# A tile ahead of the tile pools made 64 bytes longer, in a gated recurrence with a binary-weight feed-forward layer

## The chip, the cores and the metric

The kernel runs on one core of a Trainium2 chip. The metric is the time of one execution on the device in microseconds. The core's engines are TensorE (PE in the profile; its weight loads stand apart as PEld), VectorE (DVE), ScalarE (ACT), GpSimd (POOL) and SyncE (SP), which here only issues DMAs. SBUF, the memory that the engines work on, has 128 partitions; a tile takes the same range of bytes in each of them.

## The reference

The input x is [2, 4096, 256] in float32. Each of two layers is added to its input and normalised over the last axis. Cut to what matters:

```python
u = x @ W_in + b_in                       # 64 state columns
g = sigmoid(x @ W_gate + b_gate)
h_t = tanh(h_prev @ A + u_t @ Bm)         # over 4096 steps
y_t = h_t @ C.T + u_t @ D.T
y_t = g_t * y_t + (1 - g_t) * x_t
x1 = layernorm(x + (ys @ W_out + b_out + x))
# binary weights: sign(w) times the mean of |w| over a row
f = gelu(x1 @ bw1.T + b1) @ bw2.T + b2    # 256 -> 1024 -> 256
out = layernorm(x1 + f)
```

## The kernel before

**Work.** The 4096 steps of each of the two sequences are cut into 64 segments of 64 steps, so that 128 recurrences run side by side. A warm-up of 48 steps gives each segment its first state. After the run the states are compared with those that they started from; where they differ, a branch at L757 computes the recurrence one step after another and redoes all chunks. `hs`, the tile of the change, serves that branch alone.

**Chunks.** The rows are worked in 16 chunks of 512 (`N`). For each chunk the method `load` fetches `hu` (states and inputs, from `st` in SBUF) and `xn` (x, from memory); `xt` is x transposed, loaded on its own. Then follow the gate products (L313), `mix` (L370, then VectorE at L377, L382, L385), `project` (L395), the first normalisation, and `turn` (transposes at L423). `turn` splits the result into a rounded part `xhi` (ScalarE, L431) and the remainder `xlo` (VectorE, L433), both in the float32r type. `up` (L451) multiplies the signs `sg1` with both parts; the Gelu at L458 evicts the sums to `h`, which ScalarE and VectorE split again into `hhi` (L467) and `hlo` (L474). `down` (L490) uses these as weights against the signs `sg2`. The end of a chunk is `scale` (L506), `add` (L512), the second normalisation and the store (L527). An up product streams 512 columns, a down product 256. The step of the recurrence is L157 on TensorE and L158 on ScalarE; L131 makes its inputs u.

**Order.** The order of the instructions on TensorE, ScalarE, VectorE and GpSimd is written out by hand in a manual schedule. Each chunk's pieces stand among those of its neighbours, and a step of the recurrence is put in after every so many nanoseconds of planned work. SP issues nearly all DMAs, in the order of the code.

**Where tiles stand.** The pools take bytes of a partition in the order in which they are opened: `const`, `xin`, `work`, `small`. Each tile of a pool stands at a fixed byte. In the built program the `const` pool holds `st`, all weights and constants, and as its last tile `hs`; behind it come `xin` (`xt`, `hu`, `xn`), `work` (`tg`, `h`, `xhi`, `xlo`, `hhi`, `hlo`, `d`, `o`, and for a time w1, w2 and the `neg` tiles of the sign computation) and `small` (the statistics of the normalisations). A tile starts on a multiple of 32 bytes at the least. The large tiles of `const`, such as `sg1`, `sg2`, `cd`, `w_gate`, `w_out` and `wab`, start on multiples of 128 bytes.

```python
cp = ctx.enter_context(tc.tile_pool(name="const", bufs=1))
xp = ctx.enter_context(tc.tile_pool(name="xin", bufs=2))
wk = ctx.enter_context(tc.tile_pool(name="work", bufs=2))
sm = ctx.enter_context(tc.tile_pool(name="small", bufs=4))
...
hs = cp.tile([P, L + 1 + 7, B], FP, name="hs")
```

Here P is 128, L is 64 and B is 2: in each partition `hs` has 72 rows of two float32 numbers. The branch uses the first 65 of them.

Of the kernel before, what the change touches and what calls it, by code (L numbers as in the profile page):

```python
# [8 lines left out]
FP = mybir.dt.float32  # L9
# [7 lines left out]
P = 128  # L17
B, T, DM, S, H = 2, 4096, 256, 64, 1024
# [3 lines left out]
L = T // SEG  # L22
# [15 lines left out]
def gated_recurrence_then_binary_ffn(  # L38
# [18 lines left out]
    cp = ctx.enter_context(tc.tile_pool(name="const", bufs=1))  # L57
# [694 lines left out]
        do(end, "down_end")  # L752


    hs = cp.tile([P, L + 1 + 7, B], FP, name="hs")
    met = nc.values_load(flag, min_val=0, max_val=B * S * (SEG - 1))
    with tc.If(met < B * S * (SEG - 1)):  # L757
        nc.vector.memset(hs[TOP, L, :], 0.0)
# [58 lines left out]
```

## Time and profile before

| | us |
|---|---|
| median of three runs | 452.75 |
| lowest, highest | 452.65, 454.31 |
| the profiled execution | 453.36 |
| its span | 451.5 |
| TensorE busy | 439.7 |
| VectorE busy | 358.0 |
| ScalarE busy | 261.1 |
| GpSimd busy | 176.2 |

The span runs from the first instruction to the last; the profiled execution's own time holds a little more around it. Busy time is the time in which an engine had an instruction in work. Matmuls overlap in the profile, since one starts before the one ahead of it has ended; the distance from start to start tells their rate better than their length. The chain that ended last is followed back from the last instruction, at each step to what released it, and is shown in pieces of like instructions; there each piece lasts up to the start of what follows it.

### The profile page before, as it was taken

How to read it: one execution, taken by the hardware profiler on the slowest of the kernel's cores; microseconds unless marked ns; L12 is line 12 of the kernel's file. 1: busy time of each engine (PE TensorE's matmuls, PEld its weight loads, DVE VectorE, ACT ScalarE, POOL GpSimd, SP SyncE). 2: the span in 40 equal slices, each digit the busy share in tenths (PEclk: the TensorE clock that was granted, in tenths of full speed). 3: DMA queues.
4: the chain of work that ended last, by engine and by line, in shares of the span. 5: the costliest groups of instructions: out<-in, count | busy, mean ns of one | idle time of the engine just before them, and what ended most of it. 6: DMA issues, size and time to landing. Idle time of an engine off the chain costs nothing.

```text
span 451.5 us, 6729 instructions
## 1 busy us (share of the span) xinstructions
PE 439.7 (97%) x2504; PEld 357.6 (79%) x2504; DVE 358.0 (79%) x600; ACT 261.1 (58%) x424; POOL 176.2 (39%) x179
## 2 busy tenths in 40 slices
PE   8999999999999999999999999999999999989992
PEld 5665666788888888887978787979788888879982
DVE  0245737976989798989898988899898989896775
ACT  2343442485657575757574747566666656556772
POOL 1001300553545434343445454535353545451713
PEclk9999999999999999999999999999999999999997
DMA  8898814321133322322232312212112020201012
GB/s 302 267 330 305 292 36 137 102 83 23 48 105 106 107 59 94 116 94 70 93 103 70 105 52 89 76 52 67 47 37 81 13 93 1 93 1 48 1 46 100
DMA packets 14838, 44.51 MB, mean 99 GB/s; under 512 B 2000, under 2 KB 3024, under 8 KB 14800
## 3 DMA queue, kind: packets, MB, share of 16 engines
q1 hardware_dynamic: 14224, 43.65, 29.1%
q8 instruction: 22, 0.36, 0.3%
q10 hardware_dynamic: 576, 0.37, 0.3%
q14 instruction: 16, 0.13, 0.1%
HBM read 31.43 MB, written 8.39 MB: 88 GB/s over the span
## 4 chain that ended last, share of the span: by engine, by line
PE 92%; DVE 5%; DMA 1%; ACT 1%; issue 0%; POOLq 0%; POOL 0%
PE ps_h L451 25%; PE ps_o L490 24%; PE ps_z L395 12%; PE ps_g L313 12%; PE ps_y L370 6%; PE ps_s L157 6%; PE ps_u L131 4%; PE ps_t L423 3%; DMA wab<-in_W_in_AB 1%; DVE bs_b L256 1%; DVE hlo L474 1%; DVE d L382 1%; DVE d L377 1%; DVE xlo L433 1%; DVE o L506 0%; PE ps_p L490 0%
## 5 line engine op out<-in xcount | busy, mean ns | idle before, releaser
L458 ACT ACTIVATE h<-ps_h,bias_c,al 128x512 f32<-128x512 f32 x128 | 97.5, 775 | 80.4 <-PE ps_h L451 75.2
L490 PE MATMUL ps_o<-sg,hhi 128*128 128x256 f32 x496 | 120.3, 282 | 0.0
L490 PE MATMUL ps_o<-sg,hlo 128*128 128x256 f32 x496 | 119.0, 279 | 0.1
L474 DVE TENSOR_TENSOR hlo<-h,hhi 128x1024 fp32r<-128x1024 f32 (+1 forms) x65 | 84.5, 1318 | 23.6 <-ACT hhi L467 23.5
L490 PEld LDWEIGHTS ps_o<-sg,hhi 128*128 128x128 f32 x496 | 93.6, 189 | 2.3
L490 PEld LDWEIGHTS ps_o<-sg,hlo 128*128 128x128 f32 x496 | 93.4, 188 | 2.5 <-DVE hlo L474 0.3
L451 PE MATMUL ps_h<-xhi,sg 128*128 128x512 f32 x256 | 92.2, 441 | 0.0
L451 PE MATMUL ps_h<-xlo,sg 128*128 128x512 f32 x256 | 80.2, 394 | 0.2
L355 POOL TENSOR_TENSOR xn<-xn,bo_r 128x256 f32<-128x256 f32 x64 | 59.3, 957 | 48.4 <-DMA xn<-in_x 48.4
L355 POOL TENSOR_TENSOR xn<-xn,b_r 128x256 f32<-128x256 f32 x64 | 75.5, 1208 | 1.2 <-PE ps_t L423 1.2
L467 ACT CAST hhi<-h 128x1024 fp32r<-128x1024 f32 (+1 forms) x65 | 67.3, 1037 | 2.0
L313 PE MATMUL ps_g<-xt,w_gate 128*128 128x384 f32 (+3 forms) x208 | 67.9, 438 | 0.0
L266 POOL TENSOR_TENSOR rs_a<-rs_a,neg_half 128x4 f32<-128x4 f32 x16 | 17.2, 1076 | 122.2 <-DVE rs_a L265 103.4
L395 PE MATMUL ps_z<-w_out,tg 128*128 128x256 f32 x256 | 61.1, 380 | 1.5 <-DVE xlo L433 1.5
L158 ACT ACTIVATE st<-ps_s 64x128 f32<-64x128 f32 x112 | 30.0, 267 | 56.0 <-PE ps_s L157 55.6
L451 PEld LDWEIGHTS ps_h<-xlo,sg 128*128 128x128 f32 x256 | 48.1, 188 | 11.9 <-DVE xlo L433 0.9
L157 PEld LDWEIGHTS ps_s<-st,wab 128*128 128x128 f32 x224 | 38.0, 192 | 24.0 <-issue 9.9
L451 PEld LDWEIGHTS ps_h<-xhi,sg 128*128 128x128 f32 x256 | 46.1, 189 | 12.7 <-issue 6.2
L266 POOL TENSOR_TENSOR rs_b<-rs_b,neg_half 128x4 f32<-128x4 f32 (+1 forms) x19 | 19.3, 1017 | 89.2 <-DVE rs_b L265 77.0
L395 PEld LDWEIGHTS ps_z<-w_out,tg 128*128 128x128 f32 x256 | 46.0, 190 | 6.8 <-DVE xlo L433 1.7
L279 ACT ACTIVATE xn<-xn,nm_a,rs_a 128x256 f32<-128x256 f32 x60 | 31.2, 591 | 24.5 <-DVE nm_a L271 24.5
L157 PE MATMUL ps_s<-st,wab 128*128 128x128 f32 x224 | 44.6, 281 | 0.1
(73 smaller groups left out, 482.9 us busy)
## 6 DMA issues: line engine op xcount, KB each, us to landing
xt<-in_xT SPq DMA_DIRECT2D x35, 512.0 KB, 4.3
xn<-in_x SPq DMA_DIRECT2D x16, 512.0 KB, 3.4
out_y<-xn SPq DMA_DIRECT2D x15, 512.0 KB, 2.6
hu<-st SPq DMA_DIRECT2D x32, 128.0 KB, 2.3
w1t<-in_w1T SPq DMA_DIRECT2D x2, 512.0 KB, 5.9
w1n<-in_w SPq DMA_DIRECT2D x2, 512.0 KB, 6.1
w2t<-in_w2T SPq DMA_DIRECT2D x2, 512.0 KB, 4.9
xt<-in_xT SPq DMA_DIRECT2D x2, 256.0 KB, 3.5
```

Source lines behind the costliest of these rows:

```text
L157: nc.tensor.matmul(p_h, ab, st[:, j].rearrange("p b k -> p (b k)"), start=True, stop=True)
L158: nc.scalar.activation(h_of[:, j + 1].rearrange("p b k -> p (b k)"), p_h[TOP, :], AF.Tanh)
L266: nc.gpsimd.tensor_tensor(rs, rs, neg_half[:, cut], ALU.pow)
L279: nc.scalar.activation(r, r, AF.Identity, bias=self.sh[:, i : i + 1], scale=rs)
L313: nc.tensor.matmul(ps[:, cut], w_gate[:, k, bass.ts(m, P)], xt_[:, k, cut], start=k == 0 and i == 0, stop=k == KD - 1, skip_group_check=True,)
L355: nc.gpsimd.tensor_tensor(r[:, i, :], r[:, i, :], row, ALU.add)
L395: nc.tensor.matmul(self.ps_z[:, i, :], self.y[:, k, bass.ts(i, P)], w_out[:, k, :], start=k == 0, stop=k == KD - 1,)
L451: nc.tensor.matmul(ps, sg1[:, k, bass.ts(j, P)], part[:, k, :], start=n == 0, stop=n == 2 * KD - 1,)
L458: nc.scalar.activation(h[:, i, :], ps, AF.Gelu, bias=b1_c[:, j : j + 1], scale=al1[:, j : j + 1],)
L467: nc.scalar.copy(hi[:, part, :], h[:, part, :])
L474: nc.vector.tensor_sub(lo[:, i, :], h[:, i, :], hi[:, i, :].bitcast(FP))
L490: nc.tensor.matmul(ps[:, i, :], part[:, j % 2, bass.ts(tb, P)], sg2[:, j, :], start=j == 0 and part is self.h[j // 2][0] and first, stop=j ...
```

## The change

The tile `hs` gets 15 rows of padding in place of 7. It is 640 bytes long in each partition in place of 576, and all tiles of `xin`, `work` and `small` stand 64 bytes higher.

```diff
-    hs = cp.tile([P, L + 1 + 7, B], FP, name="hs")
+    hs = cp.tile([P, L + 1 + 15, B], FP, name="hs")
```

## The prediction

> **What bounds the kernel now.** I read the page's busy table and its slices first, then the chain that ended last, then the waits, then single stretches.
>
> ```profile
> PE 439.7 (97%) x2504; PEld 357.6 (79%) x2504; DVE 358.0 (79%) x600; ACT 261.1 (58%) x424; POOL 176.2 (39%) x179
> ...
> PE   8999999999999999999999999999999999989992
> ...
> DMA  8898814321133322322232312212112020201012
> ...
> PE 92%; DVE 5%; DMA 1%; ACT 1%; issue 0%; POOLq 0%; POOL 0%
> ```
>
> TensorE is busy in 97% of the span and in every slice but the last, and it is 92% of the chain that ended last. DMA is dense only in the first five slices. Busy matmul time alone proves little, since matmuls overlap; so the waits of TensorE come next.
>
> ```profile
> PE ps_z L395 <- DVE xlo L433: 1.5, 1, 1.5
> PE ps_s L154 <- POOL ones L107: 1.0, 1, 1.0
> PE ps_u L131 <- DMA wab<-in_W_in_AB: 0.4, 1, 0.4
> PE ps_y L370 <- DVE d L377: 0.2, 1, 0.2
> ```
>
> The columns are total us, times, longest us. In all, TensorE waits 3.1 us. No x tile that comes by DMA is among what it waits for, in spite of the dense first five slices. So a change must alter the rate of TensorE itself, or the few microseconds at either end, to be seen. The rate is in the pieces of the chain between 390 and 440 us (start, length, what):
>
> ```profile
> 404.90 1.89 PE ps_o L490 x16
> 408.51 1.85 PE ps_h L451 x8
> 410.36 1.84 PE ps_o L490 x16
> ...
> 430.02 3.73 PE ps_h L451 x16
> ```
>
> The same sixteen down products take 1.89 us in one piece and 1.84 us in another. Among the 34 pieces of exactly sixteen in the chain's longest pieces I count 22 of 1.89, 11 of 1.84 and one of 1.88: mean 1.8735 us, 117.1 ns a product. In the timeline of single products, starts at 414.46 and 415.14 us stand six products apart, 113.3 ns each; those at 213.16 and 214.93 us stand fifteen apart, 118.0 ns each. **TensorE has two paces** for these products, and changes between them without any wait. An up product (512 columns) takes 230.6 ns in a piece of eight at 1.845 us, and 233 ns in the piece of sixteen.
>
> **What the Trainium skill says.** "SBUF — State Buffer", section "Operand start alignment", asks only that an operand start at a multiple of its element size, and says of its runs that they "timed nothing": no price for 64 against 128 bytes. The same page, "Specifications (TRN2)", speaks of 16-byte lines; 64 and 128 are both multiples of 16, so by it no engine access changes. Its "Who interferes with whom" gives TensorE two independent read ports, moving operand and weights, and says that it never waits on anyone; the two paces show that something still costs 4.7 ns a product. "DMA: Bandwidth & Descriptors", "How a descriptor splits into AXI transactions", says that transactions start at multiples of 256 bytes. No row here shows a transaction; the 3.5 us that a first half of xt took to land is used below.
>
> **The change part by part.** The built programs place `hs` at byte 77184 of each partition in both. It is 576 bytes long before and 640 after, so `xin`, `work` and `small` begin at 77760 (607 x 128 + 64) before and at 77824 (608 x 128, also 19 x 4096) after. Tiles of `xin` and `work` take 2048 or 4096 bytes, so each starts 64 bytes past a multiple of 128 before and on one after. The statistics of `small` (slots of 96 and 32 bytes) keep mixed starts, whatever the title says. The `const` tiles do not move. Every engine's and queue's list of instructions has the same order: nothing is removed, added or moved past anything, SP's and POOL's included, and no wait is added.
>
> (1) `hs` itself is used only in the branch at L757, which did not run: no row of the profile has a line of it. Cost 0.
>
> (2) TensorE's reads. The kernel before already holds both cases. The down products stream `sg2` (a `const` tile, on a multiple of 128) against weights from `hhi`/`hlo` (64 past one); the up products stream `xhi`/`xlo` (64 past) against weights from `sg1` (on one). Per 512 columns the first are 2 x 117.1 = 234.2 ns, or 226.6 at the fast pace; the second 230.6. The tiles 64 past are not slower. Weight loads take the same from either:
>
> ```profile
> L490 PEld LDWEIGHTS ps_o<-sg,hhi 128*128 128x128 f32 x496 | 93.6, 189 | 2.3
> ...
> L451 PEld LDWEIGHTS ps_h<-xhi,sg 128*128 128x128 f32 x256 | 46.1, 189 | 12.7 <-issue 6.2
> ```
>
> So I take 0, by the nearest rows. What the trace does not hold is an up or down product with both of its streams on multiples of 128. Bounds for that: all down products at the fast pace give 64 sixteens x (1.8735 - 16 x 0.1133) = 3.9 us less; all at the slow pace 64 x (1.89 - 1.8735) = 1.1 us more, and all up products at 233 ns another 512 x 2.4 ns = 1.2 us, together 2.3 us more.
>
> (3) VectorE, ScalarE, GpSimd. VectorE gives the pair to compare:
>
> ```profile
> L195 DVE TENSOR_SCALAR nega<-w1t 128x512 f32<-128x512 f32 x4 | 1.7, 420 | 0.0
> ...
> L188 DVE TENSOR_SCALAR w_out<-w_out 128x512 f32<-128x512 f32 x1 | 0.4, 427 | 0.0
> ```
>
> 420 ns on pool tiles against 427 on a `const` tile, of one size: no gain from a multiple of 128. ScalarE's casts take 1051 ns for 1024 elements and 616 for 512, 0.85 ns an element, and VectorE's `hlo` row of 512 takes 688 ns, 1.34 ns an element with its start. There is no such pair for ScalarE or GpSimd; were each 5% off either way, it would lie under TensorE, whose products wait 1.7 us in all for VectorE and never for ScalarE. I take 0, and 0.3 us either way for the tail after 440 us, where VectorE is the chain. If TensorE's cover were gone, 5% of VectorE's 358 us would be 18 us, but 358 is 94 us under the span.
>
> (4) Transfers. By the skill's rule a row of 4096 bytes that starts 192 bytes past a multiple of 256 touches 17 blocks and an aligned one 16: an estimate of 6% of the moving part. The rule is told of reads; for writes into the pools I bound it by 0 and 6%. Loads lie under TensorE; the exceptions are the first `xt`, for which the weight load at L131 waited 0.2 us (3.5 us to land, 6% would be 0.2), and the last stores of 128 KB (2.6 us to land). I take 0.1 us less, between 0 and 0.4.
>
> **Sum:** 0 + 0 + 0 - 0.1. The profiled execution took 453.36 us, 451.5 of it span; that gives 453.3. It stands 0.6 us over the median of three (452.75), so beside the median I predict 452.6.
>
> **The rivals.** *Faster, by the pace.* The weights and the moving rows of one product both start on a multiple of 128, and the slow pace, if it is two reads of unlike phase getting in each other's way, goes: 452.75 - 3.9 = 448.9 us. For it: two paces exist and no wait explains them. Against it: both occur with the same unlike phases. *Faster, by the line.* If reads come in 128-byte lines, 512 columns touch 17 lines before and 16 after: 230.6/17 = 13.6 ns x 512 up products = 6.9 us, 445.8 us. Against it: the down products' aligned rows are no quicker per column. *Slower.* The two ports of TensorE now begin in the same phase in every up and down product and clash: place L451 and L490, price all at the slow pace, 455.1 us; another half of the 4.7 ns step on 1024 down products adds 2.4, so 455.1 to 457.5, at 456.3. It decides once the mean product costs 1.5 ns more (2.3 us over 1536). For it: today all these products pair a tile on 128 with one 64 past. Against it: the step products at L157 pair `st` with `wab`, both on 128, and their row has 281 ns where the gate products of 128 columns at L313 (`xt`, 64 past) have 280; but these are float32 products, at about twice the time a column (four of 512 columns at L370 are 1.72 us of the chain). *The change does not do what it says:* that is so for `small`, but at 0 us.
>
> **How the numbers follow.** No effect 0.42 (its own range 451.5 to 454.0), faster 0.30 (0.18 by the pace, 0.12 by the line), slower 0.28. About 0.5% (2.3 us) is what a measurement of this kernel can tell from no change; the two sides stay high because their prices are larger than that and the trace has no product of the new kind. The range 447.0 to 457.0 leaves out most of the line case and the slower case's upper end, some 0.15.
>
> **What would show it.** Right: pieces of sixteen still at 1.84 and 1.89 in about one to two, pieces of eight at 1.85, the same four waits of TensorE. Wrong: sixteens all at 1.81, eights at 1.74 or all at 1.87 and more, or a wait of TensorE over 1 us that is not in the list above.

## The result and the profile after

The changed kernel takes 456.12 us (median of six runs, 455.17 to 457.20) where the kernel before takes 453.20 (six runs). The ratio is 1.0063, with a 95% interval of 1.0048 to 1.0078: 2.9 us more, between 2.2 and 3.5. Its profiled execution took 457.2 us, 455.4 of it span.

The page of the changed kernel, the lines that answer to those of before:

```profile
PE 443.3 (97%) x2504; PEld 360.7 (79%) x2504; DVE 358.6 (79%) x600; ACT 261.3 (57%) x424; POOL 174.5 (38%) x179
...
PE   8999999999999999999999999999999999989992
...
DMA  8798814311132312322242213111121020201002
...
PE 92%; DVE 5%; DMA 1%; ACT 0%; issue 0%; POOL 0%; POOLq 0%
```

TensorE has the same 2504 products and the same share of the span, but is busy 3.6 us longer; VectorE's 0.6 us and ScalarE's 0.2 us more are small beside that. Its waits, in the same columns as before:

```profile
PE ps_z L395 <- DVE xlo L433: 1.3, 1, 1.3
PE ps_s L154 <- POOL ones L107: 1.0, 1, 1.0
PE ps_u L131 <- DMA wab<-in_W_in_AB: 0.5, 1, 0.5
PE ps_y L370 <- DVE d L377: 0.2, 1, 0.2
```

They are the same four waits, 3.0 us in all. So TensorE does not wait longer; it works more slowly. The chain between 390 and 440 us (start, length, what) shows where:

```profile
405.76 1.85 PE ps_h L451 x8
407.61 1.91 PE ps_o L490 x16
...
413.11 1.92 PE ps_o L490 x16
...
433.24 3.71 PE ps_h L451 x16
```

The sixteens of 1.83 and 1.84 us are gone. The chain has 47 pieces of exactly sixteen down products. After the change 4 of them take 1.89 us, 14 take 1.90, and 29 take 1.91 to 1.93. Before it 13 take 1.83, 11 take 1.84, one takes 1.88 and 22 take 1.89; two of those of 1.83, which the prediction's count leaves out:

```profile
414.04 1.83 PE ps_o L490 x16
...
418.58 1.83 PE ps_o L490 x16
```

To measure this better, the starts of the products were taken from the trace: the mean distance from one start to the next inside a group of like products. Distances over 130 ns (down) or 260 ns (up), nearly all at the start of a group, are left out; 937 and 375 distances remain in each kernel. A down product (L490) takes 116.1 ns before and 119.2 after, an up product (L451) 230.6 and 232.4. That makes 1024 x 3.1 + 512 x 1.8 ns = 4.1 us, against 3.9 us between the two spans and 2.9 us between the medians.

Weight loads, and the pair of VectorE rows that compared pool tiles with a `const` tile, are as they were:

```profile
L490 PEld LDWEIGHTS ps_o<-sg,hhi 128*128 128x128 f32 x496 | 93.5, 189 | 2.4
...
L451 PEld LDWEIGHTS ps_h<-xhi,sg 128*128 128x128 f32 x256 | 46.1, 189 | 12.7 <-issue 6.2
```

```profile
L195 DVE TENSOR_SCALAR nega<-w1t 128x512 f32<-128x512 f32 x4 | 1.7, 420 | 0.0
...
L188 DVE TENSOR_SCALAR w_out<-w_out 128x512 f32<-128x512 f32 x1 | 0.4, 427 | 0.0
```

The `neg` tiles moved by 64 bytes and still take 420 ns.

### The profile page after: what moved, and what is told of

It is laid out like the page before. It is cut to its first block, busy times and chain, and to the rows that moved or that the text cites. A ratio compares the mean times of both kernels' runs of the same rounds, so it can differ in the third digit from the quotient of the medians.

```text
span 455.4 us, 6729 instructions
## 1 busy us (share of the span) xinstructions
PE 443.3 (97%) x2504; PEld 360.7 (79%) x2504; DVE 358.6 (79%) x600; ACT 261.3 (57%) x424; POOL 174.5 (38%) x179
## 4 chain that ended last, share of the span: by engine, by line
PE 92%; DVE 5%; DMA 1%; ACT 0%; issue 0%; POOL 0%; POOLq 0%
PE ps_h L451 25%; PE ps_o L490 25%; PE ps_z L395 12%; PE ps_g L313 12%; PE ps_y L370 6%; PE ps_s L157 6%; PE ps_u L131 4%; PE ps_t L423 3%; DMA wab<-in_W_in_AB 1%; PE ps_p L490 1%; DVE bs_b L256 1%; DVE d L382 1%; DVE d L377 1%; DVE xlo L433 1%; DVE o L506 0%; DVE xn L512 0%
## 5 line engine op out<-in xcount | busy, mean ns | idle before, releaser
L490 PE MATMUL ps_o<-sg,hhi 128*128 128x256 f32 x496 | 123.0, 285 | 0.0
L490 PE MATMUL ps_o<-sg,hlo 128*128 128x256 f32 x496 | 121.8, 283 | 0.0
L490 PEld LDWEIGHTS ps_o<-sg,hlo 128*128 128x128 f32 x496 | 93.5, 189 | 2.6 <-DVE hlo L474 0.2
L490 PEld LDWEIGHTS ps_o<-sg,hhi 128*128 128x128 f32 x496 | 93.5, 189 | 2.4
L451 PE MATMUL ps_h<-xhi,sg 128*128 128x512 f32 x256 | 92.5, 442 | 0.0
L451 PE MATMUL ps_h<-xlo,sg 128*128 128x512 f32 x256 | 80.7, 395 | 0.2
L355 POOL TENSOR_TENSOR xn<-xn,bo_r 128x256 f32<-128x256 f32 x64 | 57.9, 935 | 45.6 <-DMA xn<-in_x 45.6
L451 PEld LDWEIGHTS ps_h<-xlo,sg 128*128 128x128 f32 x256 | 48.2, 188 | 12.1 <-DVE xlo L433 0.9
L157 PEld LDWEIGHTS ps_s<-st,wab 128*128 128x128 f32 x224 | 37.9, 192 | 24.2 <-issue 10.4
L451 PEld LDWEIGHTS ps_h<-xhi,sg 128*128 128x128 f32 x256 | 46.1, 189 | 12.7 <-issue 6.2
L157 PE MATMUL ps_s<-st,wab 128*128 128x128 f32 x224 | 44.5, 281 | 0.1
```

Source lines behind the costliest of these rows:

```text
L157: nc.tensor.matmul(p_h, ab, st[:, j].rearrange("p b k -> p (b k)"), start=True, stop=True)
L355: nc.gpsimd.tensor_tensor(r[:, i, :], r[:, i, :], row, ALU.add)
L451: nc.tensor.matmul(ps, sg1[:, k, bass.ts(j, P)], part[:, k, :], start=n == 0, stop=n == 2 * KD - 1,)
L490: nc.tensor.matmul(ps[:, i, :], part[:, j % 2, bass.ts(tb, P)], sg2[:, j, :], start=j == 0 and part is self.h[j // 2][0] and first, stop=j ...
```

## The experiments

Below, the **distance** of a product is the first byte of its weights minus the first byte of its moving rows, modulo 256. With the places in the built programs, before: pools at 192 modulo 256, `sg1` and `sg2` at 128, so 192 - 128 = 64 in the down products and 128 - 192, that is 192, in the up products. After: pools at 0, so 128 in both. All tiles are moved by padding alone, and padding holds no data that is read. Each ratio compares a run with the kernel before, run again beside it. Added lines shift the numbers in the traces: L491 and L492 are the down products of L490.

### Pools on other multiples

```diff
-    hs = cp.tile([P, L + 1 + 7, B], FP, name="hs")
+    hs = cp.tile([P, L + 1 + 23, B], FP, name="hs")
```

> hs gets 23 rows of padding, so all pool tiles start 128 bytes above those of before: again 64 past a multiple of 128, but 64 past a multiple of 256 where before they are 192 past one. Phase theory (a product whose weights and moving rows start in the same 128-byte phase is slower; only the place within 128 bytes counts): as before, 453.2 us within 1, sixteens of L490 at 1.84 and 1.89. Rival (a period of 256 bytes, or any move of the pools that costs): 455 us or more, sixteens of 1.90 to 1.92.

Measured: 455.12 us, ratio 1.0056 (1.0036 to 1.0076). L490 takes 117.5 ns and L451 233.4. The pools stand 64 past a multiple of 128, as before, and the loss is nearly that of the change; here the up products carry half of it. So the place within 128 bytes does not decide, and a start on a multiple of 128 is not what costs. With +11 in place of +23:

> hs gets 11 rows of padding: pool tiles start 96 past a multiple of 128. Phase theory: they differ in phase from sg1 and sg2 (on multiples of 128), so about as before, 453 to 454 us. Rival (the absolute start counts: reads from a start that is no multiple of 64 touch one more 64-byte line): slower than both, over 457 us, with up products (L451) over 232 ns as well.

Measured: 455.50 us, ratio 1.0062 (1.0042 to 1.0081), L490 118.2 ns, L451 233.6. It meets neither expectation: the kernel is slower than before, but no slower than the one that starts on multiples of 128.

### Moving sg2 alone

```diff
-    sg1 = cp.tile([P, KD, H], FR, name="sg1")
+    sg1_room = cp.tile([P, KD * H + 16], FR, name="sg1")
+    sg1 = sg1_room[:, : KD * H].rearrange("p (k h) -> p k h", k=KD)
```

`hs` has 7 rows of padding, so the pools stand where the change puts them.

> Pool tiles stay on multiples of 128 as in the changed kernel; sg1's tile is 64 bytes longer, so that sg2 and the small constants behind it start 64 past a multiple of 128. The down products (L490) then pair weights on 128 with moving rows 64 past; the up products (L451) keep both on 128. Phase theory: L490 goes back to the mean of before, sixteens of 1.84 and 1.89, which returns 3.2 of the 3.7 us: 453.5 us. Rival (weights or pool tiles on multiples of 128 cost by themselves): stays at 456, sixteens of 1.90 to 1.92.

Measured: 451.92 us, ratio 0.9980 (0.9966 to 0.9995): 0.2% faster than before, and by the two ratios 0.8% faster than the changed kernel, with the pools on multiples of 256 as there. L490 takes 114.6 ns, L451 232.5, nearly as in the changed kernel. From its chain:

```profile
199.97 1.82 PE ps_o L491 x16
...
205.59 1.83 PE ps_o L491 x16
```

Moving the other partner of the down products takes away more than the whole loss of the down products. For them it is the pair of places that counts, not the place of the pools.

### TensorE alone

```python
for n, count in ((256, 32), (512, 16)):    # down-like, up-like
    for a, wo in zip(NAMES, OFF):          # the weights' place
        for c, mo in zip(NAMES, OFF):      # the moving rows' place
            ...                            # a new PSUM tile ps for the block
            for i in range(count):
                nc.tensor.matmul(ps[:, :n], w[:, bass.ds(wo // 4 + i % 4 * P, P)],
                                 m[:, bass.ds(mo // 4, n)], start=i == 0, stop=i == count - 1)
```

> Leaves the whole computation out. TensorE alone runs 36 blocks of 32 down-like float32r products (256 columns) and 36 of 16 up-like ones (512 columns), with the weights starting 0, 32, 64, 96, 128 and 192 bytes past a multiple of 128 (letters a to f after w) and the moving rows likewise (letters after m). Phase theory: blocks with equal phase modulo 128 (aa, ae, ea, ee, bb, cc, cf, fc, ff, dd) are at about 119 ns a product of 256 columns, the others at 113 to 117. Rival (the two paces come from other engines' accesses): all blocks alike, at 113 ns.

Measured: with the other engines still (VectorE and GpSimd busy for 0 us between 25 and 125 us), the place makes as large a difference as in the kernel, so other engines' accesses are not needed for it. But equal phase against unlike phase is not the rule: of 36 down blocks, only three settle at 113.4 ns (weights at 64, 128 and 192 with moving rows 64 bytes lower), and the rest at 117 to 120. Two blocks of the same distance, 64 modulo 256, are among the rest, at 117.8 (weights at 0 with moving rows at 192, and 96 with 32). The blocks with equal places are the fastest of the up ones; they settle at 227 to 228 ns. A second run of the kind used the kernel's own order of addresses and more places:

> Leaves the whole computation out. Blocks of 32 down-like and 16 up-like float32r products in the very order of addresses that the kernel uses (two parts 4096 bytes apart, steps of 512 within the weights, 1024 or 2048 in the moving rows), weights starting at 0 (wa) or 64 (wc), moving rows at 16 places from 0 to 960 (letters a to p: 0, 32, 64, 96, 128, 192, 256, 320, 384, 448, 512, 576, 832, 960, 16, 48), and float32 blocks (f) of 256 columns. Distance theory: down blocks are at 113 ns only where the weights start 64 bytes after the moving rows, modulo 256 or 512: wa with m at 192, 448, 960 (mod 256) or only 448 and 960 (mod 512), wc with m at 0, 256, 512; others 117 to 120. Up blocks 227 to 229 at distance 0 or with the moving rows 64 after the weights, else 233. Float32 blocks all at 216. Rival (equal against unlike phase within 128 bytes): only two values, by m minus w modulo 128.

Its chain, whose pieces are the blocks of 32 down products (`d`) and 16 up products (`u`):

```profile
30.03 3.80 PE ps_dwame L85 x32
33.83 3.77 PE ps_dwamf L85 x32
37.60 3.84 PE ps_dwamg L85 x32
41.44 3.77 PE ps_dwamh L85 x32
...
49.01 3.66 PE ps_dwamj L85 x32
...
135.68 3.63 PE ps_uwama L85 x16
...
143.04 3.67 PE ps_uwamc L85 x16
...
194.80 3.73 PE ps_uwcma L85 x16
```

The letters stand for distances: down `ame` 128, `amf` 64, `amg` 0, `amh` 192, `amj` 64; up `ama` 0, `amc` 192, `cma` 64. Once a block has settled (its second half), the trace's starts give these times by distance:

| distance | down product, ns | up product, ns |
|---|---|---|
| 0 | 120 | 227 |
| 64 | 113.4 or 117.8 | 233 |
| 128 | 118.7 | 233 |
| 192 | 117.8 | 229 |

With weights at 64, moving rows at 0, 256 and 512 give the same: 113.4, 113.3 and 113.4 ns. With weights at 0, moving rows at 0 and 128 do not: 120.0 and 118.7. So the period is 256 bytes in all that was tried, apart from the two paces of distance 64. There four of the six down blocks settle at 113.4 ns and two stay at 117.8 for all 32 products. These two came directly after a block of distance 128 and one of distance 192; but three of the four fast ones (`amj`, `cmg`, `cmk`) came after blocks of distance 128 as well, so the distance of the block ahead does not alone decide. The other distances settle into patterns that repeat to about a nanosecond, and none of them is at 113. The eight float32 blocks all take 215.8 ns a pass.

### All in one phase, and what the up products do

`hs` with 15 rows and `sg1` 64 bytes longer, as in the edits above, put both partners of the down products 64 past a multiple of 128:

> hs has 15 rows of padding and sg1's tile is 64 bytes longer: all pool tiles and sg2 start 64 past a multiple of 128, none of them on one; sg1 stays on one. The distance from sg2 to the down weights is that of the changed kernel (128 modulo 256). Distance theory: L490 at 119 ns as in the changed kernel, about 456 us. Rival (a start on a multiple of 128 is what costs): 453 us or less.

Measured: 456.74 us, ratio 1.0074 (1.0057 to 1.0091), L490 119.2 ns as in the changed kernel. The up products, now at distance 64, take 233.2. In this trace TensorE also waits 1.9 us for transfers of `xt` and `hu`, which it does not in the changed kernel; the time of a product does not hold that wait.

`w_out`'s tile lengthened by 80 numbers and `sg1`'s by 48 moves `sg1` alone, modulo 512; with 112 numbers for `sg1`'s and 39 rows for `hs`, `sg2` moves as well:

> Pools and sg2 stand as in the kernel before, modulo 512; w_out's tile and sg1's tile are longer, so that sg1 starts at the same place modulo 512 as xhi and xlo (distance 0 in the up products, -64 before modulo 256). Distance theory: L451 goes from 230.6 to about 227 to 229 ns, 512 products, 1 to 1.8 us less: 451 to 452 us, with L490 as before. Rival (up products do not feel the place; their 1 ns in the changed kernel was a side effect): 452.7.

Measured: 453.49 us, ratio 1.0009 (0.9998 to 1.0019); L490 116.9 ns, L451 230.9. The gain did not come: at distance 0 the up products ran at 227 ns alone, but in the kernel they mostly come in pieces of eight, and the starts show some five products of 224 to 236 ns before the pattern settles.

> As the run with sg1 at the place of xhi modulo 512, and sg2 moved so that hhi and hlo start 64 bytes after it modulo 512 (before: 64 modulo 256, 320 modulo 512). Distance theory with a period of 512: L490 goes from 116.1 to about 113.5 ns, 1024 products, 2.7 us less, besides 1 to 1.8 us of L451: 448.2 to 449 us. With a period of 256: only the part of L451, 451 to 452 us. Rival of the order (the two paces of L490 are set by what runs ahead of each sixteen): 451 to 453.

Measured: 453.45 us, ratio 1.0010 (1.0000 to 1.0020), L490 116.8 ns, L451 231.0. In the down products a distance of 64 modulo 512 is no better than one of 320, which agrees with the period of 256; the gain of the up products fails here too.

### The loss undone, and one half alone

```diff
-    w_out = cp.tile([P, KD, DM], FP, name="w_out")
+    w_out_room = cp.tile([P, KD * DM + 16], FP, name="w_out")
+    w_out = w_out_room[:, : KD * DM].rearrange("p (k d) -> p k d", k=KD)
```

> The pools stay where the change put them, on multiples of 128 bytes. w_out's tile is 64 bytes longer and hs as long as before, so that sg1 and sg2 move up with the pools: weights start 64 bytes after the moving rows in the down products and 192 in the up products (modulo 256), as before. Distance theory: the whole loss is gone, 453.0 us within 0.7, sixteens of 1.84 and 1.89, eights of 1.84 and 1.85. Rival (something else that stands in the pools is slower on multiples of 128: transfers, GpSimd, ScalarE): 455.5 to 456.5.

Measured: 452.92 us, ratio 0.9991 (0.9978 to 1.0004). L490 takes 116.1 ns as before, and both paces are back (26 of 47 sixteens at 1.83 or 1.84 us, 21 at 1.89). L451 takes 231.5 where it took 230.6 before at the same distance; that 0.9 ns is not explained.

```profile
199.95 1.84 PE ps_o L491 x16
...
205.55 1.89 PE ps_o L491 x16
```

All pool tiles stand where the change put them, and the loss is gone. So the place of the pools by itself, for the transfers and the other engines, costs nothing that shows. With `sg2` moved on until its distance is that of the changed kernel again (`sg1` 48 numbers longer, `hs` 15 rows):

> Pools on multiples of 256; sg1 moved so that the up products have the distance of before (192), sg2 such that the down products have that of the changed kernel (128). Distance theory: L490 at 119 ns, L451 at 230.6: 3.1 us more than before, 456.1 us. Rival (both families lose only together): under 455.

```profile
201.48 1.91 PE ps_o L492 x16
...
207.16 1.91 PE ps_o L492 x16
```

Measured: 455.77 us, ratio 1.0057 (1.0040 to 1.0075), L490 119.1 ns, L451 230.7. The down products alone carry most of the loss: 3.1 of the 4.1 us by the starts, and by the times the two ratios (1.0057 and 1.0063) are not told apart.

The last two runs keep distance 64 in the down products and change the up products' (`w_out` 32 and `sg1` 32 numbers longer; `w_out` 8 and `sg1` 56):

> Pools and sg2 as before modulo 256 (distance 64 in the down products); sg1 moved so that the up products have distance 64, where they ran alone at a steady 233 ns. Distance theory alone: L451 costs 512 x 2.6 ns = 1.3 us more. Which of its two paces L490 takes depends on what runs ahead of each sixteen: 113.5 throughout would give 2.7 us back (451.7 us), 117.8 throughout cost 1.7 more (456.1 us).

Measured: 453.32 us, ratio 1.0004 (0.9996 to 1.0013), L490 115.3 ns, L451 233.0.

> As the run before, with distance 224 in the up products (moving rows 32 bytes after the weights), where they ran alone in the pattern 235, 230, 236, 234, 231. L451 at 233 ns, 1.2 us more; L490 at a pace between 113.5 and 117.8: between 451.5 and 456 us. The theory of two paces set by what runs ahead needs another share of the fast pace in this run than in the one before; the rival (the share is the same whatever runs ahead) has 116.1 ns in both.

Measured: 454.50 us, ratio 1.0028 (1.0016 to 1.0041), L490 116.9 ns, L451 232.7. From the chain of the first and of the second:

```profile
218.11 1.82 PE ps_o L492 x16
```

```profile
219.46 1.89 PE ps_o L492 x16
```

In the first 32 of the 47 sixteens take 1.82 or 1.83 us, in the second 11. The down products' places are the same in these two, 1.6 ns lie between them, and the two ratios lie apart: the up products ahead of a sixteen help to decide which pace it takes.

All kernels together:

| kernel | distance down, up | L490, L451 ns | ratio to before |
|---|---|---|---|
| before | 64, 192 | 116.1, 230.6 | 1 |
| changed | 128, 128 | 119.2, 232.4 | 1.0063 |
| +23 rows | 192, 64 | 117.5, 233.4 | 1.0056 |
| +11 rows | 96, 160 | 118.2, 233.6 | 1.0062 |
| sg2 moved | 64, 128 | 114.6, 232.5 | 0.9980 |
| both 64 past | 128, 64 | 119.2, 233.2 | 1.0074 |
| sg1 at xhi's place | 64, 0 | 116.9, 230.9 | 1.0009 |
| the same, sg2 too | 64, 0 | 116.8, 231.0 | 1.0010 |
| loss undone | 64, 192 | 116.1, 231.5 | 0.9991 |
| down half alone | 128, 192 | 119.1, 230.7 | 1.0057 |
| up at 64 | 64, 64 | 115.3, 233.0 | 1.0004 |
| up at 224 | 64, 224 | 116.9, 232.7 | 1.0028 |

The sum 1024 x L490 + 512 x L451 of the profiled executions ranks the kernels nearly as the ratios do, but its differences from the kernel before lie 0.2 to 1.2 us above those of the times: 4.1 us against 2.9 for the changed kernel, 4.4 against 3.4 for "both 64 past". Those two executions were 1.1 and 1.2 us slower than their kernel's median. Each kernel has one trace, so how far the shares of the two paces differ from run to run is not shown. But the two pairs of kernels with equal distances agree in L490 within 0.2 ns (116.1 and 116.1, 116.9 and 116.8).

## Why the prediction was wrong

**What bounds the kernel** held. TensorE's rate is the time, the four waits are the same, and nothing of DMA, VectorE, ScalarE or GpSimd came onto the path. The part on transfers cannot be told from nothing: `xt` lands in 3.9 us where it took 4.3, under TensorE, and its first half in 3.6 where it took 3.5.

**The step that failed is (2), TensorE's reads, taken at 0 "by the nearest rows".** In its place the starts show 3.1 ns more for each down product and 1.8 for each up product, 4.1 us together. The rows were compared by where each tile stands against a multiple of 128. Both families take about the same time a column, and I read from this that the place does not matter. But the families stood at two particular distances, 64 and 192, and the change moved both to a third one, 128, of which the trace held nothing. The text said so, and still gave the case without an effect the most chance. The two paces could not have settled it, since both occur at one and the same place; that the fast one is to be had at distance 64 alone came only with the runs of TensorE alone. The range of 447.0 to 457.0 does hold 456.12, but it was drawn wide for rivals of both signs, and its value stood for no effect.

**One reading behind its bounds was wrong too.** The 34 sixteens came from a list of the chain's longest pieces, and the list ended above the shortest sixteens: the 13 of 1.83 us are missing. With all 47 the mean is 1.8615 us, 116.3 ns a product, not 117.1. The bounds become 64 x (1.8615 - 16 x 0.1133) = 3.1 us less and 64 x (1.89 - 1.8615) = 1.8 us more, or 3.0 with the up products. The bounds of (2) held no pace slower than 1.89 us a sixteen, and neither did the prediction's signs of being right or wrong.

**The slower rival was right in place and sign**: L451 and L490, 455.1 to 457.5 us with 456.3 as its value, against 456.12. How close it came is in part luck: with the full count its range would have been 455.8 to 458.2, that is 3.0 to 5.4 us more than before, where 2.9 were measured. Its point of decision was 1.5 ns a product; measured are (1024 x 3.1 + 512 x 1.8) / 1536 = 2.7. Its reason was only half right. Two starts in one phase of 128 bytes are not what costs: the run with +23 rows has unlike phases and loses nearly as much, and equal places are the best of all for up products alone. What counts is the distance modulo 256. Nor is the cost one slow pace throughout: 43 of the 47 sixteens of the changed kernel, at 1.90 to 1.93 us, are slower than the slow pace of before. The objection to this rival, from the float32 products at L157, said nothing of float32r, as the float32 blocks show.

**The faster rivals fell.** The changed kernel loses the fast pace instead of keeping to it, and up products that start on a multiple of 128 got slower, not faster. No run reached the fast pace throughout; with `sg2` moved, L490 is 1.5 ns under before and the kernel 0.2% faster.

**Two readings of the Trainium skill** need a word beside the measurements. "SBUF — State Buffer", section "Who interferes with whom", calls TensorE's two read ports independent. Here, with every other engine still, the time of a product follows from the distance between what the two ports read. And the 16-byte lines of the same page, section "Specifications (TRN2)", from which the prediction took that no access changes between 64 and 128, do not explain it: the measured period is 256 bytes.

## What to carry to other kernels

Where TensorE bounds a kernel and its float32r products load new weights each time, as here, look at the starts of the products for more than one pace, and work out the distance from weights to moving rows modulo 256 bytes. A pad of 64 bytes ahead of one of the two tiles is worth a try: a down product took 113 to 120 ns by its place, and the kernels here ran from 0.2% faster to 0.7% slower than before. "Aligned" tells nothing by itself: the same pool places gave 451.9 and 456.1 us. When counting pieces of a chain, make sure that the list holds the short ones. A pad at the end of one pool moves every tile behind it, so a change that seems to touch one small tile is an edit of all pairs across that border.

## What was not expected of the hardware

The times of products follow exact patterns: at distance 128, down blocks repeat 115, 118, 122, 120, 119 ns, within a nanosecond, for as long as they run. At distance 64 two paces both last, and what ran ahead helps to choose between them. What inside TensorE or SBUF makes a period of 256 bytes was not tried.

Float32 products do not feel the place: 215.8 ns a pass of 256 columns in all eight blocks, about half the rate of the float32r ones. Each of them stands in the trace as two passes, so a float32 product of 256 columns takes 432 ns, nearly four times a float32r one. The prediction's "twice the time a column" counted passes as products.
